# The experts' preparation at the ends of the last layer: by pairs of sequences, or by half sequences

## The chip, the cores and the metric

The kernel runs on one core of one Trainium2 chip. The metric is the device time of one execution in microseconds (us). The kernel before took 1163.84 us, the median of three runs (1162.24 to 1168.53). The profile is of another single execution, which took 1141.5 us.

## What is computed

Eight sequences (B = 8) of 512 tokens with 128 channels pass a modulated LayerNorm, four layers of a Mamba-2 block, a residual, a second modulated LayerNorm and a mixture of experts. Cut to what matters here:

```
h = layernorm(x) * (1 + ca) + sa
for l in range(4):                      # four Mamba-2 layers
    h = h + mamba2(rmsnorm(h), l)       # its scan runs along the 512 tokens
x = x + ga * rmsnorm(h)                 # final norm: scale F
h = layernorm(x) * (1 + cb) + sb        # scale L
normed = rmsnorm(h)                     # scale G
probs = sigmoid(normed @ router_w.T)    # 8 experts, the best 2 of each token
out = shared(normed) + routed(normed, probs)   # two-layer networks, hidden size 512
x = x + gb * out
```

The three scales F, L and G are powers of -1/2 of a mean or a variance over the 128 channels of a token. They, the two norms between them and the modulation are what the change moves.

## The kernel before, in words

**The layers.** A sequence is cut into four chunks of 128 tokens (NC = 4). An item i is one chunk of one sequence in one layer: NI = 128 items, the last layer's sequence b holding items 96 + 4b to 96 + 4b + 3. One loop over t, from -25 to 131, carries all items as a software pipeline written out by hand: in iteration t it does stage k of item t + k for each stage. So item i has its decay rows loaded in iteration i - 4 (`decay_rows`), their difference and mask made on GpSimd in i - 3 (`decay_diff`, L801, and `decay_mask`, L806), its exponential on ScalarE in i - 2, its products weighed on GpSimd in i - 1 (L844, L847), its state decayed on GpSimd in i (L894). `gate` follows in i + 1, `out_scale` and `project_out` in i + 2, and `out_add` in i + 3. The last two take the items by twos: after an odd item `out_scale` makes the gate norm's scale of both chunks (L966 on VectorE, then the power at L967 on GpSimd), and `out_add` (L975, VectorE) adds both projected chunks to the residual h. The new units' projections and convolutions run 16 iterations ahead, so they end at t = 112. From there on `drain` is true.

**The order of the work.** Each engine works through its queue in order, and this order is fixed when the kernel is built: inside the loop on all engines by `manual_schedule`; after the loop on all engines but GpSimd, whose instructions a planner places. Generators (`gens`) hold the side work: each `yield` ends a step. In every iteration each generator takes one step near the end of the iteration; in the drain those with a tuple as key take a further one in `step_pairs`, ahead of `gate`.

**The ends of the layers.** The generator `rejoin(g)` handles a pair of sequences, 2g and 2g + 1, eight chunks. It starts in iteration 106 + 8g, in which `out_add` finishes the pair's last chunks: at t = 106, 114, 122 and 130. In order, and with [128 x 128] pieces unless said otherwise:

- the modulation's rows `md` come by two DMAs on SyncE (L328);
- eight squares with their sums on ScalarE (`mean_squares`, L312), the mean (L316) and the power F;
- eight copies scaled by F on ScalarE (L343), a product with `md` per sequence (L347) and one sum into x (L349) on VectorE;
- statistics on VectorE (L355, L357), the power L, the offset (L365);
- eight scaled and shifted copies on ScalarE (L368), product and sum with `md` on VectorE (L375);
- eight squares (L312) and the power G.

These are 18 steps. In eleven more follow: the rows (eight copies scaled by G, L385), transposes (L394), the router's product (L402), its sigmoid (L424), the choice of two experts and the positions in the experts' lists on VectorE (L427 to L480), and then 16 scatters of 128 rows each are put on a list. `power` (L297 to L305) computes the three powers: on GpSimd in one instruction for pairs 0 and 1, on VectorE in eleven small ones for pairs 2 and 3.

**Scatters and the shared network.** `scatter` (L487) is an indirect DMA from GpSimd's queue, 64 of them for the rows of all tokens. In the drain one is taken from the list per iteration, while t is at most 124; the loop after the layers takes all that are listed. `shared`, stepped by `serve`, computes the shared network (L529 to L562): six steps per sequence as soon as the sequence is routed, one in each iteration of the drain, three in each round after the loop. The rows of pair 0 and 1 lie in a pool of two buffers; a third pair may not take one inside the loop while scatters of pair 0 are listed (`held`), so that pair 2's rows wait for the loop's end.

**After the loop.** Rounds step the remaining generators twice each, list the scatters and `serve` three times. When all four pairs have counted their tokens, `tables` works out which expert owns which tile of 256 rows. Then the experts' loop reads the rows back (L1188) and works through 39 tiles. Its first read waits for the last scatter.

Of the kernel before, what the change touches and what calls it, by code (L numbers as in the profile page):

```python
# [8 lines left out]
F32 = mybir.dt.float32  # L9
I32 = mybir.dt.int32  # L10
AF = mybir.ActivationFunctionType
ALU = mybir.AluOpType
# [3 lines left out]
P = 128  # L16
# [8 lines left out]
def adaln_mamba_moe(  # L25
# [49 lines left out]
    small = ctx.enter_context(tc.tile_pool(name="small", bufs=4))  # L75
    norm = ctx.enter_context(tc.tile_pool(name="norm", bufs=4))
# [13 lines left out]
    hs = {}  # L90
# [16 lines left out]
    unread = const.tile([P, DM], F32, name="unread")  # L107
    mhalf = const.tile([P, 2 * NC], F32, name="mhalf")
# [5 lines left out]
    scb = const.tile([P, B, P], F32, name="scb")  # L114
# [98 lines left out]
    hTs, hp, xp, xs = {}, {}, {}, {}  # L213


    G2 = 2 * NC
# [19 lines left out]
    mods = lists.tile([B, 4, DM], F32, name="mods")  # L236
# [52 lines left out]
    sets = [(b, b + 1) for b in range(0, B, 2)]  # L289
    routed = set()  # L290

    def power(v, name, on_pool):

        n = v.shape[1]
        y = small.tile([P, G2], F32, tag="py", name=f"py{name}")[:, :n]
        if on_pool:
            nc.gpsimd.tensor_tensor(y, v, mhalf[:, :n], ALU.pow)  # L297
            return y
        t = small.tile([P, G2], F32, tag="pt", name=f"pt{name}")[:, :n]
        nc.vector.tensor_single_scalar(t.bitcast(I32), v.bitcast(I32), 1, ALU.arith_shift_right)  # L300
        nc.vector.tensor_scalar(y.bitcast(I32), t.bitcast(I32), -1, 0x5F3759DF, ALU.mult, ALU.add)
        for _ in range(3):
            nc.vector.tensor_mul(t, y, y)
            nc.vector.scalar_tensor_tensor(t, t, -0.5, v, ALU.mult, ALU.mult)
            nc.vector.scalar_tensor_tensor(y, t, 1.5, y, ALU.add, ALU.mult)  # L305
        return y

    def mean_squares(h, eps, name, on_pool):
        n = h.shape[1]
        ss = small.tile([P, G2], F32, tag="pss", name=f"pss{name}")[:, :n]  # L310
        for j in range(n):
            nc.scalar.activation(unread, h[:, j, :], AF.Square, accum_out=ss[:, j : j + 1])  # L312
            if j % NC == NC - 1:
                yield
        v = small.tile([P, G2], F32, tag="pv", name=f"pv{name}")[:, :n]
        nc.vector.tensor_scalar(v, ss, 1.0 / DM, eps, ALU.mult, ALU.add)  # L316
        return power(v, name, on_pool)

    def rejoin(g):


        seqs = sets[g]
        b0, n = seqs[0], len(seqs) * NC
        parts = [slice(i * NC, (i + 1) * NC) for i in range(len(seqs))]
        md = []
        for b in seqs:
            md.append(norm.tile([P, NC, DM], F32, tag="hn", name=f"md{b}"))
            nc.sync.dma_start(  # L328
                md[-1].rearrange("p k d -> p (k d)"), mods[b].rearrange("k d -> (k d)").partition_broadcast(P)
            )  # L330

        def both(k):

            for i, t in enumerate(parts):
                yield t, md[i][:, k, :].unsqueeze(1).to_broadcast([P, NC, DM])

        mine = slice(b0 % 2 * NC, b0 % 2 * NC + n)
        h, xt = (v[b0 // 2].rearrange("p b s d -> p (b s) d")[:, mine] for v in (hp, xp))
        on_pool = g < 2
        rs = yield from mean_squares(h, 1e-5, f"F{g}", on_pool)  # L340
        yield
        for j in range(n):
            nc.scalar.activation(h[:, j, :], h[:, j, :], AF.Copy, scale=rs[:, j : j + 1])  # L343
            if j % NC == NC - 1:
                yield
        for t, m in both(0):
            nc.vector.tensor_mul(h[:, t, :], h[:, t, :], m)  # L347
        yield
        nc.vector.tensor_add(xt, xt, h)  # L349
        yield  # L350
        mv = small.tile([P, G2, 2], F32, tag="pmv", name=f"mvF{g}")[:, :n]
        for i in range(len(seqs)):
            st = small.tile([P, NC, 6], F32, tag="st", name=f"stF{g}_{i}")
            for s in range(NC):
                nc.vector.bn_stats(st[:, s, :], xt[:, i * NC + s, :])  # L355
            for s in range(NC):
                nc.vector.bn_aggr(mv[:, i * NC + s, :], st[:, s, :])  # L357
            yield
        v = small.tile([P, G2], F32, tag="pv", name=f"pvL{g}")[:, :n]
        nc.vector.tensor_scalar_add(v, mv[:, :, 1], 1e-5)  # L360
        rs = power(v, f"L{g}", on_pool)
        if on_pool:
            yield
        off = small.tile([P, G2], F32, tag="poff", name=f"off{g}")[:, :n]
        nc.vector.scalar_tensor_tensor(off, mv[:, :, 0], -1.0, rs, ALU.mult, ALU.mult)  # L365
        yield
        for j in range(n):
            nc.scalar.activation(  # L368
                h[:, j, :], xt[:, j, :], AF.Identity, bias=off[:, j : j + 1], scale=rs[:, j : j + 1]
            )  # L370
            if j % NC == NC - 1:
                yield
        for k in (2, 1):
            for t, m in both(k):
                nc.vector.tensor_tensor(h[:, t, :], h[:, t, :], m, ALU.mult if k == 2 else ALU.add)  # L375
            yield
        rs = yield from mean_squares(h, 1e-8, f"G{g}", on_pool)
        yield

        while scatters and scatters[0][0] in held.get(len(rowpools), [])[:-1]:  # L380
            yield
# [8 lines left out]
        for i, b in enumerate(seqs):  # L390
            t = parts[i]
# [21 lines left out]
        def t3(tag):  # L413
            return f2.tile([P, G2, E], F32, tag=tag, name=f"{tag}{g}")[:, :n]
# [7 lines left out]
        m = n * E  # L422
        p = t3("prob")
# [29 lines left out]
        src, w = before, 1  # L453
        while w < n:
# [3 lines left out]
            src, w = dst, 2 * w  # L458
# [119 lines left out]
    with ExitStack() as actx:  # L578
# [13 lines left out]
        U = NL * B  # L592
        NI = U * NC
        n = NC * NH
# [3 lines left out]
        dV, Ms, xTs, xds, xes, pg, py, st, gs, sqs, po = ({} for _ in range(11))  # L598
# [364 lines left out]
        def out_scale(i):  # L963
            if i % 2:
                rs = small.tile([P, 2], F32, tag="rg", name=f"rg{i}")
                nc.vector.tensor_scalar(rs, po[i // 2][:, 2 * DM : 2 * DM + 2], 1.0 / DI, 1e-5, ALU.mult, ALU.add)  # L966
                nc.gpsimd.tensor_tensor(rs, rs, mhalf[:, 0:2], ALU.pow)  # L967
                po[i // 2] = po[i // 2], rs

        def out_add(i):  # L970
# [22 lines left out]
        gens = {}  # L993
# [9 lines left out]
        for t in range(-NC * LEAD - EARLY, NI + 4):  # L1003
            p = t + NC * LEAD
# [16 lines left out]
            for g, seqs in enumerate(sets):  # L1021
                if t == NC * (U - B) + NC * (seqs[-1] + 1) + 2:
                    gens["pairs", g] = rejoin(g)
            v, j = divmod(p, NC)
            vc, jc = divmod(p - 1, NC)

# [52 lines left out]
            if item(t - 2):  # L1079
                out_scale(t - 2)  # L1080
# [153 lines left out]
    with tc.manual_schedule(engines={*tc.nc.engines} - {mybir.EngineType.Pool}):  # L1234
# [39 lines left out]
        for b in range(B):  # L1274
            both = xbp.tile([P, NX, L], F32, tag="xbc", name=f"y{b}") if b % 2 == 0 else both
# [7 lines left out]
        for b in range(B):  # L1283
# [3 lines left out]
            y = y1[b].rearrange("p (s d) -> p s d", d=DM)  # L1287
# [56 lines left out]
```

## Time and profile before

| what | us |
|---|---|
| median of three runs | 1163.84 |
| profiled execution, its own time | 1141.5 |
| its span, first to last instruction | 1139.8 |
| iteration 100 begins on GpSimd (L801 of item 103) | 672.43 |
| iteration 112 (item 115) | 738.44 |
| iteration 124 (item 127, the last) | 829.88 |
| scale of the last two chunks begins (L966) | 867.70 |
| last `out_add` (L975) | 872.35 |
| last scatter begins | 948.96 |
| first rows read back | 951.97 |

The times of the iterations are read off GpSimd's timeline: L801 of item i is issued in iteration i - 3, and item 127 is its last. Lines of the trace's answers give a start or a duration in us, the engine (PE TensorE, PEld its weight load, DVE VectorE, ACT ScalarE, POOL GpSimd, SP SyncE), the output by its name in the program, and the line of the kernel. A wait reads "engine output line <- releaser: us in all, times, longest". The lines themselves stand in the prediction.

### The profile page before, as it was taken

To read this page: it belongs to the slowest core of one execution; us is meant where nothing else is said; L and a number is where in the kernel's file an instruction comes from. 1 tells how busy PE (TensorE), PEld (TensorE's weight loads), DVE (VectorE), ACT (ScalarE), POOL (GpSimd) and SP (SyncE) were. 2 spreads that over 40 slices of the span, in tenths; PEclk is the share of its full clock that TensorE was granted. 3 is DMA by queue.
4 is the path that set the end of the run, shared out by engine and by line. 5 is a ranking of instruction groups with operands and counts; after the bars stand their busy time and mean duration, and the time that the engine had idled before them with its cause. 6 is when DMAs were issued, how large, how long until landed. Compare 5 with 4: busy or idle time off the path is not lost. (4 is left out here: it accounts for less than half of the span.)

```text
span 1139.8 us, 21562 instructions
## 1 busy us (share of the span) xinstructions
PE 960.9 (84%) x7130; PEld 730.6 (64%) x7130; DVE 855.0 (75%) x2084; ACT 761.4 (67%) x1641; POOL 856.1 (75%) x937
## 2 busy tenths in 40 slices
PE   4757899989999989899998998988666985999995
PEld 1335676767667667676666676666454674888882
DVE  3768888898888978988889889888764652666653
ACT  4766888878888888788878887876624731333320
POOL 6868879898898898988988988879756163555550
PEclk9777999999999999999999999978876996999998
DMA  5141436556466364563332433434201015878756
GB/s 111 5 139 39 138 100 199 138 167 169 137 194 170 115 195 141 169 184 107 111 120 78 141 111 125 130 94 139 84 24 37 11 55 162 218 223 229 221 147 228
DMA packets 134302, 151.19 MB, mean 133 GB/s; under 512 B 22568, under 2 KB 106696, under 8 KB 134192
## 3 DMA queue, kind: packets, MB, share of 16 engines
q1 hardware_dynamic: 127184, 137.91, 41.5%
q0 software_dynamic: 4672, 9.42, 2.4%
q10 hardware_dynamic: 2336, 2.50, 0.7%
q8 instruction: 56, 0.92, 0.3%
q14 instruction: 54, 0.44, 0.1%
HBM read 120.07 MB, written 29.71 MB: 131 GB/s over the span
## 5 line engine op out<-in xcount | busy, mean ns | idle before, releaser
L668 DVE SCALAR_TENSOR_TENSOR xbc<-px,cw,xbc 128x511 f32<-128x511 f32 (+2 forms) x384 | 286.3, 746 | 35.7 <-ACT xbc L658 28.6
L801 POOL TENSOR_TENSOR dV<-dV,cum 128x1024 f32<-128x1024 f32 x128 | 244.7, 1912 | 4.5 <-DMA dV<-crow 4.3
L860 DVE TENSOR_TENSOR dV<-dV,ptx 128x1024 f32<-128x1024 f32 x128 | 155.0, 1211 | 19.7 <-ACT xT L838 19.7
L806 POOL TENSOR_SCALAR_AFFINE_SELECT dV<-dV 128x1024 f32<-128x1024 f32 x128 | 142.2, 1111 | 9.3
L817 ACT ACTIVATE dV<-dV 128x1024 f32<-128x1024 f32 x128 | 134.5, 1051 | 14.8 <-POOL dV L806 14.5
L487 POOL DMA_INDIRECT yg<-y,ix x78 | 84.1, 1078 | 79.4 <-DVE y L1230 64.8
L944 ACT ACTIVATE sq<-g 128x256 f32<-128x256 f32 x128 | 53.0, 414 | 115.5 <-DVE g L940 104.4
L646 PE MATMUL px<-hT,Wi 128*128 128x512 f32 x192 | 103.8, 622 | 15.8 <-DVE xbc L668 14.5
L658 ACT ACTIVATE xbc<-px,cbias,cw 128x512 f32<-128x512 f32 x128 | 98.6, 770 | 14.6 <-PE px L646 13.4
L487 POOL DMA_INDIRECT xg<-row,ix x64 | 63.0, 984 | 50.3 <-ACT hds L529 29.6
L844 POOL TENSOR_TENSOR xd<-xT,dt 128x256 f32<-128x256 f32 x128 | 79.4, 621 | 26.9 <-ACT xT L838 26.5
L869 PEld LDWEIGHTS py<-xbc,st 128*128 128x128 f32 x384 | 58.9, 200 | 61.3 <-issue 47.0
L959 PE MATMUL po<-Wo,g 128*128 128x128 f32 x512 | 89.4, 298 | 0.0
L1212 ACT ACTIVATE hd<-ph,bs 128x256 f32<-128x256 f32 x78 | 32.8, 471 | 83.7 <-PE ph L1206 81.2
L928 PE MATMUL py<-dV,xd 128*32 128x128 f32 x2048 | 84.6, 284 | 0.0
L955 PEld LDWEIGHTS po<-ones,sq 128*128 128x128 f32 x512 | 68.0, 193 | 25.6 <-issue 23.7
L918 PEld LDWEIGHTS py<-xbc,dg 128*128 128x128 f32 x512 | 78.4, 199 | 6.8 <-issue 1.0
L856 PE MATMUL ptx<-xbc 128*128 128x128 f32 x256 | 55.6, 299 | 31.7 <-DVE dV L860 31.3
L918 PE MATMUL py<-xbc,dg 128*128 128x128 f32 x512 | 80.5, 281 | 0.0
L955 PE MATMUL po<-ones,sq 128*128 128x1 f32 x512 | 78.4, 257 | 0.0
L1219 PE MATMUL pe<-w,hd 128*128 128x128 f32 x624 | 75.9, 275 | 0.0
L1206 PE MATMUL ph<-xt,w 128*128 128x256 f32 x312 | 75.5, 386 | 0.0
(252 smaller groups left out, 2342.5 us busy)
## 6 DMA issues: line engine op xcount, KB each, us to landing
dV<-crow SPq DMA_DIRECT2D x128, 512.0 KB, 4.2
w<-in_L_ffn_ew_dram SPq DMA_DIRECT2D x78, 256.0 KB, 3.3
xg<-blank SPq DMA_DIRECT2D x64, 260.0 KB, 4.6
ecum<-crow SPq DMA_DIRECT2D x256, 48.0 KB, 3.2
rows<-xg SPq DMA_DIRECT2D x39, 130.0 KB, 3.7
b<-in_L_ffn_eb_dram SPq DMA_DIRECT2D x39, 64.0 KB, 4.0
x<-in_L_attn_x_dram SPq DMA_DIRECT2D x8, 256.0 KB, 9.4
md<-mods SPq DMA_DIRECT2D x8, 256.0 KB, 4.3
```

What stands on the lines that cost most here:

```text
L487: i = nc.gpsimd.indirect_dma_start(out=to, out_offset=bass.IndirectOffsetOnAxis(ap=ix, axis=0), in_=of, in_offset=None)
L646: nc.tensor.matmul(px[v, k][:, :L], Wi[l][:, c0 : c0 + P], hT[v], start=True, stop=True)
L658: nc.scalar.activation(xbc[v][:, k, :], px[v, k][:, :L], AF.Identity, bias=cbias[:, l, k : k + 1], scale=cw[:, l, k, KT - 1 : KT],)
L668: nc.vector.scalar_tensor_tensor(xbc[v][:, k, d:], px[v, k][:, : L - d], cw[:, l, k, KT - 1 - d : KT - d], xbc[v][:, k, d:], ALU.mult, ALU ...
L801: nc.gpsimd.tensor_tensor(dV[i], dV[i], cums[g][:, h0 : h0 + NH].unsqueeze(2).to_broadcast([P, NH, Q]), ALU.subtract)
L806: nc.gpsimd.affine_select(out=dV[i], in_=dV[i], pattern=[[0, NH], [1, Q]], compare_op=ALU.is_ge, fill=-200.0, base=0, channel_multiplier=-1,)
L817: nc.scalar.activation(dV[i], dV[i], AF.Exp)
L860: nc.vector.tensor_mul(Ms[i], Ms[i], pg.pop(i).unsqueeze(1).to_broadcast([P, NH, Q]))
L918: nc.tensor.matmul(py[i][:, k, :], dg[l][:, k, :], xbc[u][:, k, t], start=False, stop=True, skip_group_check=True,)
L928: nc.tensor.matmul(py[i][j * HD : (j + 1) * HD, k, :], xd[:, h, :], M[:, h, :], start=False, stop=True, skip_group_check=True,)
L955: nc.tensor.matmul(pp[:, 2 * DM + c : 2 * DM + c + 1], sq[:, k, :], ones[:, 0:1], start=(k == 0), stop=(k == NB - 1))
L959: nc.tensor.matmul(pp[:, c * DM : (c + 1) * DM], g[:, k, :], Wo[l][:, k, :], start=(k == 0), stop=(k == NB - 1))
```

## The change

The first two thirds of `rejoin`, up to the power G, become a generator of their own, `half(b, k)`, for two chunks (half a sequence). It starts in the iteration of the `out_add` that finishes these two chunks: half n = 2b + k starts at t = 100 + 2n, for n = 0 to 15. `rejoin(g)` still starts where it did, but first waits until the pair's four halves are `ready`, and then goes on with the rows. A half has eleven steps. Its key is a tuple as well, so that in the drain it takes two per iteration.

In a half, the copies scaled by F and the products with `md` become one VectorE instruction per chunk (`scalar_tensor_tensor`), the sum into x has 256 columns, and so have product and sum with `md`. The small results lie in columns of `scb`, a tile that is free by then. The powers go to GpSimd for sequences 0 to 5 and to VectorE for 6 and 7 (before: 0 to 3, and 4 to 7); the offset is made on GpSimd in two instructions for all sequences (before: one on VectorE). `md` is loaded per sequence with its first half. `out_scale` of the last two odd items (125, 127) takes its power on VectorE.

The core of the diff:

```
+    def half(b, k):
+        if k == 0:
+            mds[b] = norm.tile([P, NC, DM], F32, tag="hn", name=f"md{b}")
+            nc.sync.dma_start(
+                mds[b].rearrange("p k d -> p (k d)"), mods[b].rearrange("k d -> (k d)").partition_broadcast(P)
+            )
+        two = slice(2 * k, 2 * k + 2)
+        h, xt = hs[b][:, two, :], xs[b][:, two, :]
...
+        def power_of(v, name, to=None):
+            if b < B - 2:
+                to = few() if to is None else to
+                nc.gpsimd.tensor_tensor(to, v, mhalf[:, :2], ALU.pow)
+                return to
+            rs = power(v, f"{name}{b}_{k}")
+            if to is not None:
+                nc.vector.tensor_copy(to, rs)
+            return rs
+
+        ss, v = few(), few()
+        sums(ss)
+        yield
+        nc.vector.tensor_scalar(v, ss, 1.0 / DM, 1e-5, ALU.mult, ALU.add)
+        yield
+        rs = power_of(v, "F")
+        yield
+        for j in range(2):
+            nc.vector.scalar_tensor_tensor(
+                h[:, j, :], h[:, j, :], rs[:, j : j + 1], mds[b][:, 0, :], ALU.mult, ALU.mult
+            )
+        nc.vector.tensor_add(xt, xt, h)
+        yield
...
+        for j in range(2):
+            nc.vector.bn_stats(st[:, j, :], xt[:, j, :])
+        for j in range(2):
+            nc.vector.bn_aggr(mv[:, j, :], st[:, j, :])
+        v, off = few(), few()
+        nc.vector.tensor_scalar_add(v, mv[:, :, 1], 1e-5)
+        yield
+        rs = power_of(v, "L")
+        nc.gpsimd.tensor_mul(off, mv[:, :, 0], rs)
+        nc.gpsimd.tensor_scalar_mul(off, off, -1.0)
+        yield
+        for j in range(2):
+            nc.scalar.activation(
+                h[:, j, :], xt[:, j, :], AF.Identity, bias=off[:, j : j + 1], scale=rs[:, j : j + 1]
+            )
+        yield
+        nc.vector.tensor_mul(h, h, both(2))
+        nc.vector.tensor_add(h, h, both(1))
+        yield
+        ss, v = few(), few()
+        sums(ss)
+        yield
+        nc.vector.tensor_scalar(v, ss, 1.0 / DM, 1e-8, ALU.mult, ALU.add)
+        yield
+        power_of(v, "G", scales(b)[:, two])
+        ready.add((b, k))
...
     def rejoin(g):
...
+        while not all((b, k) in ready for b in seqs for k in range(2)):
             yield
...
-                nc.gpsimd.tensor_tensor(rs, rs, mhalf[:, 0:2], ALU.pow)
+                if i < NI - 4:
+                    nc.gpsimd.tensor_tensor(rs, rs, mhalf[:, 0:2], ALU.pow)
+                else:
+                    rs = power(rs, f"g{i}")
...
+            last = t - 3 - NC * (U - B)
+            if 0 <= last < NC * B and last % 2:
+                gens["half", last] = half(last // NC, last % NC // 2)
```

More of the change, by code (lines that the diff above doesn't have):

```diff
@@ L290, in adaln_mamba_moe, with power @@
     routed = set()
-    def power(v, name, on_pool):
+    scratch = scb.rearrange("p b q -> p (b q)")
+    mds, ready = {}, set()
+    def power(v, name):
         n = v.shape[1]
         y = small.tile([P, G2], F32, tag="py", name=f"py{name}")[:, :n]
-        if on_pool:
-            nc.gpsimd.tensor_tensor(y, v, mhalf[:, :n], ALU.pow)
-            return y
         t = small.tile([P, G2], F32, tag="pt", name=f"pt{name}")[:, :n]
@@ L306, in power, with few, both, sums @@
         return y
[L308 to L317, printed above, removed]
+    def half(b, k):
[6 more added lines that the diff above has]
+        h, xt = hs[b][:, two, :], xs[b][:, two, :]
+        at = [24 * (2 * b + k)]
+        def few(w=2):
+            at[0] += w
+            return scratch[:, at[0] - w : at[0]]
+        def both(row):
+            return mds[b][:, row, :].unsqueeze(1).to_broadcast([P, 2, DM])
+        def sums(ss):
+            for j in range(2):
+                nc.scalar.activation(unread, h[:, j, :], AF.Square, accum_out=ss[:, j : j + 1])
+        def power_of(v, name, to=None):
[20 more added lines that the diff above has]
+        yield
+        st = small.tile([P, NC, 6], F32, tag="st", name=f"stF{b}_{k}")
+        mv = few(4).rearrange("p (s m) -> p s m", m=2)
+        for j in range(2):
[9 more added lines that the diff above has]
+        yield
+        for j in range(2):
+            nc.scalar.activation(
[12 more added lines that the diff above has]
+        ready.add((b, k))
@@ L319, in rejoin, with scales @@
+    def scales(b):
+        return scratch[:, 24 * 2 * B + NC * b : 24 * 2 * B + NC * (b + 1)]
     def rejoin(g):
@@ L324, in rejoin @@
         parts = [slice(i * NC, (i + 1) * NC) for i in range(len(seqs))]
[L325 to L357, printed above, removed]
-            yield
-        v = small.tile([P, G2], F32, tag="pv", name=f"pvL{g}")[:, :n]
@@ L360, in rejoin @@
[L360 to L378, printed above, removed]
+        h = hp[b0 // 2].rearrange("p b s d -> p (b s) d")
+        rs = scratch[:, 24 * 2 * B + NC * b0 : 24 * 2 * B + NC * b0 + n]
+        while not all((b, k) in ready for b in seqs for k in range(2)):
+            yield
         while scatters and scatters[0][0] in held.get(len(rowpools), [])[:-1]:
```

## The prediction

> **What bounds the kernel now.** First I read the busy time by stage, cut at the iterations' starts: iterations 92 to 100, 100 to 106, 106 to 112, 112 to 124, 124 to the end of the layers, from there to the last index of the scatters, and to the first rows read back.
>
> ```profile
> core 0: us, PE busy (x) PEld busy (x) DVE busy (x) ACT busy (x) POOL busy (x), PEclk, DMA share, GB/s
> 627.23:672.43 45.20, 41.70 (x355) 31.54 (x353) 39.74 (x85) 38.30 (x77) 39.47 (x44) 1.00 0.35 113
> 672.43:704.17 31.74, 29.36 (x237) 21.72 (x236) 26.70 (x56) 26.75 (x43) 29.04 (x33) 1.00 0.49 154
> 704.17:738.44 34.27, 32.80 (x284) 24.96 (x282) 29.75 (x60) 28.65 (x63) 29.71 (x31) 0.95 0.36 111
> 738.44:803.59 65.15, 50.49 (x415) 40.38 (x414) 56.84 (x132) 44.70 (x123) 58.20 (x55) 0.84 0.41 130
> 803.59:829.88 26.29, 15.57 (x101) 11.24 (x102) 18.05 (x58) 15.63 (x51) 19.91 (x20) 0.81 0.14 48
> 829.88:872.35 42.47, 31.00 (x197) 24.64 (x196) 21.01 (x87) 13.89 (x44) 25.61 (x29) 0.72 0.09 29
> 872.35:928.97 56.62, 48.11 (x262) 34.00 (x263) 30.20 (x146) 36.47 (x96) 21.14 (x22) 0.88 0.08 27
> ```
>
> The reader is to see two regimes. Up to 803.59 VectorE and GpSimd are both busy 84 to 91% of the time, with no room for much more. After that every engine but TensorE has room. Next the chain of waits, in order of time, at the end of the layers:
>
> ```profile
> 872.35 0.61 DVE h L975 x2
> ...
> 880.61 1.28 ACT h L343 x4
> ...
> 909.52 1.28 ACT row L385 x4
> ...
> 928.34 0.70 ACT hds L529
> ...
> 929.32 0.96 POOL xg L487
> ...
> 948.96 3.00 DMA xg<-row,ix
> 951.97 2.10 DMA rows<-xg
> ```
>
> From the last `out_add` to the first rows read back takes 951.97 - 872.35 = 79.6 us, all on pair 3's way: 37 us of preparation (872.35 to 909.52), 20 of routing, 20 of 16 scatters (1.26 us from start to start), 3 until the last has landed. Last, the waits from 872 to 952:
>
> ```profile
> POOL xg L487 <- ACT hds L529: 29.6, 2, 25.6
> ACT row L385 <- DVE pyG L305: 7.9, 2, 7.5
> DVE h L975 <- POOL rg L967: 4.5, 1, 4.5
> ```
>
> GpSimd stands idle for 25.6 us between the scatters of pair 1 and of pair 2, and VectorE loses 4.5 us on the last power, which stood behind scatters (GpSimd's timeline has ten of them from 858.20 on ahead of L967 at 871.57). The rows of pair 2 wait behind that, and PE starves for a bank until 878.55.
>
> **What the Trainium skill says.** "VectorE: DVE Perf Modes", section "The TRN2 errata — SBUF-src ops pay a fixed extra latency per instruction", prices an fp32 sum or product of N columns at (N + 151)/0.96 ns: 691 ns for 512, where the trace has 641 to 1810 (L375, median 686). I take its 424 ns for 256 columns (an estimate), twice for each half where one instruction had 512 or 1024. "GPSIMD Engine Reference", "Specifications", says that GpSimd and VectorE share SBUF interfaces and contend when a VectorE instruction has two SBUF inputs. The trace agrees: L347, two such inputs, took 691 to 2093 ns, and L801 rose from 1.90 to 2.34 us beside it. "Perfetto Trace Analysis", "DMA Instruction — SWDGE (GPSIMD)", says that the end shown for an indirect DMA is that of its descriptors, not of the data: the 3.00 us on the chain after the last 0.96 us scatter are that.
>
> **The change part by part.**
>
> One half costs, by rows of before. VectorE: three small ones at 0.17, two `scalar_tensor_tensor` of 128 columns at 0.31 (L975 has 0.30 to 0.35), three 256-column ones at 0.42, statistics 0.65 (half of L355 and L357, 0.87 + 0.37), one more 0.17: 3.2 us. ScalarE: four squares with their sums at 0.44 (start to start), two copies at 0.41: 2.6. GpSimd: three powers of two columns at 0.70 (L967), product 0.20 and sign 0.23 (L177, L178): 2.5. For b = 6, 7 the powers are on VectorE: 3 x 2.25 = 6.8 more (eleven instructions, 873.07 to 875.32), and 0.43 on GpSimd. The pairs of before cost GpSimd 4.9 each (3 x 1.64) for pairs 0 and 1 only; VectorE 8.2 uncontended, 11 to 13 with the contention seen. ScalarE loses 32 copies, 12 us, all of it beside other work.
>
> *A, t = 100 to 112 (672.4 to 738.4, 66.0 us).* Six halves begin and take a step per iteration. By 112 they have done 12 us on VectorE, 10 on GpSimd, 11 on ScalarE, where before pair 0's first six steps put 2, 1.6 and 7.3. Added: 10 + 8 + 3 = 21 us. How much shows? Pair 0's own steps give the rate: 11 us of them over six iterations went with 34.27 - 31.74 = 2.5 us, or 0.23 per us. So 21 x 0.23 = **+5 us** (0 if they fall in gaps; 10 if VectorE, then 66.5 us busy, is the bound at 88%). The `md` loads, now one per four iterations on SyncE ahead of the decay rows, cost 0.43 us of issue each and land in 4.3; their buffers are long free, and the rows they stand before are wanted three iterations later: nothing, or 0.4 each if that lead were gone.
>
> *B, t = 112 to 124 (738.4 to 829.9, 91.5 us).* GpSimd is busy 78.1. Five powers of 1.64 go (-8.2), the rest of the 12 halves comes (30.4 - 9.8 - 1.8 = 18.8): 88.7 us. Pair 0 is routed 3.5 to 4 iterations sooner (step 29 was at t = 123, is at 119), so up to seven more of its scatters fall here (8.8): at most 97.5. VectorE: 75 us minus 23 (preparation of pairs 0 and 1) plus 21 to 29 for halves and 8.5 for pair 1's routing: 81 to 89. At 94% of GpSimd's time this stage is 94 to 104 us: +3 to +12. I take **+6** (bounds 0 and +18).
>
> *C, t = 124 to the last scale (829.9 to 867.7).* VectorE has 21 of 42 us. Pair 2's preparation and pair 1's routing leave (some 14), the powers of halves 12 to 14 and of `out_scale` come (some 25): 32 us, fits. Seven scatters may have left, among which L894 waited 6.6 us (VectorE's timeline, 837.16), and pair 1's 16 come in. **-3** (bounds -10, +6).
>
> *D, from L966 of items 126 and 127 on (867.70 to 951.97, 84.3 us).* The last scale takes 2.25 us on VectorE in place of 4.5: `out_add` ends at +3.1. Half 15 then needs 1.0 (squares), 2.6 (mean, power), 1.1, 1.0, 2.3, offset 0.9, copies 1.5, 0.9, squares 1.2, 2.6: rows at about +19, where before they began at 909.52, which is +42. Routing, with TensorE working off the shared network between (three serves per round, 7.25 us per six: eight sequences' matmuls from the trace; 24 of them ahead of pair 3's positions, plus 5): index at +37, before +61. This is no longer last. Pair 2 keeps its place (its rows still wait for the end of the loop), but not behind VectorE's stall: with its 11 steps and 15 serves its index is at +22 (before +37, at 905). Then 32 scatters at 1.26 = 40, landing and read 5: rows at +67.5. **-17** (-10 if pair 2's index stays at +29; -22 if only pair 3 counts: 37 + 20 + 5 = 62). All 48 serves done by then: four more fall in the loop, 33 x 1.21 + 6 = 46 us.
>
> Sum: 5 + 6 - 3 - 17 = **-9 us** on the 1141.5 of the profiled execution: 1132.5, a ratio of 0.992. The median shown is 22 us above that execution, a gap that nothing in the page explains; I carry the ratio over: 1163.84 x 0.992 = 1154.6 us. The experts' loop after 952 is untouched.
>
> **The rivals.** Half a per cent, 5.8 us, is about what a measurement of this kernel can tell from no change.
>
> *The halves hide.* A and B grow by 0 to 2 us, as the pieces are shorter and let the items' work between them (a product of 3.54 us for two instructions, at 768.99, is gone); then -20: 1143.5. For it: 46 us of VectorE's 200 are idle from 672 to 872. Against: the two regimes above.
>
> *Pair 2's scatters are last and come no sooner.* If its index stays near 905, at +37, the end is +37 + 40 + 5 = +82, and D gains 2; with +4 from A to C that is +2: 1166. It speaks for it that pair 2's rows keep their place in the program; against it that they stood waiting for VectorE from 868.
>
> *GpSimd is the bound before t = 124* (the slower side). It must then do 66.9 us in A and 97.5 in B, 164.4 us. If it can't exceed the 89% of 738 to 804, A and B last 185 in place of 157.5: +27; C gives back 5, D 14: +8, or 1172. Price: 30 small operations' us against 9.8 before, in a queue which each item passes three times. It decides once the last `out_add` is more than 17 us later.
>
> **How the numbers follow.** The likeliest case, A to D as summed: 0.42, its own range 1147 to 1160. The halves hide: 0.22. Pair 2's scatters: 0.18. GpSimd the bound: 0.18. Faster by over 0.5% are the second and most of the first (0.36): 0.58. Within: 0.06 and most of the third: 0.22. Slower: 0.20. The range goes from 1138 (hidden, and a D of -25) to 1172, the middle of the slower case; about 0.18 lies outside.
>
> **What would show it.** In the profile after: item 127's L801 at about 841 (829.88 before), L975's last at about 878; no wait of it for L967; pair 3's rows within 25 us of it; GpSimd's gap before pair 2's scatters under 15 us; 32 scatters nearly on end; rows at about 943. It is wrong if L975's last is past 889, or if GpSimd idles before pair 3's scatters.

## The result, and the profile after

The changed kernel takes 1193.76 us in the median of 4 runs (1192.64 to 1196.02), the kernel before 1165.78 us beside it (4 runs, 1162.24 to 1168.53): a ratio of 1.0244, 95% interval 1.0208 to 1.0281. It is slower by 28 us, where 9 us less were forecast. The profiled execution of the change took 1192.96 us, span 1190.3, close to its median; that of before lay 24 us below its median, so the two profiles stand 50 us apart where the medians stand 28. The experiments below ran on five chips, beside a kernel before of 1145 to 1147 us (the last two: 1167), and each ratio is to the runs of before beside it.

Busy time by stage in the changed kernel, cut at the same marks as before: iterations 100, 106, 112, 122, 124, the last `out_add`, the last index of the scatters.

```profile
core 0: us, PE busy (x) PEld busy (x) DVE busy (x) ACT busy (x) POOL busy (x), PEclk, DMA share, GB/s
672.56:707.42 34.86, 31.71 (x240) 23.00 (x239) 30.73 (x66) 29.32 (x56) 32.00 (x38) 0.95 0.44 144
707.42:750.77 43.35, 35.98 (x280) 26.52 (x278) 40.15 (x99) 29.81 (x71) 35.98 (x45) 0.88 0.32 101
750.77:842.93 92.16, 63.79 (x452) 50.60 (x452) 70.63 (x189) 47.93 (x134) 77.69 (x94) 0.74 0.31 101
842.93:858.81 15.88, 9.51 (x65) 6.47 (x65) 13.54 (x25) 6.18 (x14) 13.77 (x17) 0.71 0.03 9
858.81:914.08 55.27, 34.61 (x199) 24.60 (x199) 39.72 (x172) 15.64 (x49) 26.62 (x35) 0.69 0.06 21
914.08:976.42 62.34, 44.81 (x247) 33.86 (x248) 30.05 (x164) 24.68 (x61) 16.39 (x20) 0.80 0.05 18
```

All stages but the fourth are longer: 34.9, 43.4, 92.2, 55.3 and 62.3 us, where before had 31.7, 34.3, 65.2, 42.5 and 56.6. The fourth, t = 122 to 124, has 15.9 us in place of 26.3: nine of pair 0's scatters stood in it before, and 14 of the 16 now stand in the third. VectorE, which had 21 of 42 us in the fifth, now has 40 of 55. Next the chain of waits at the end, in order of time, and the waits after the last `out_add`.

```profile
913.91 0.52 DVE h L995 x2
...
924.15 1.17 ACT row L402 x4
...
953.46 14.75 another core or an unknown queue
968.22 0.57 ACT h L550
...
974.71 0.22 PE pos L479 x2
...
1002.79 3.27 DMA rows<-xg
```

```profile
ACT h L550 <- remote: 33.0, 2, 18.3
POOL xg L504 <- DVE ix L497: 18.2, 1, 18.2
DVE rest L489 <- PE pos L479: 17.6, 2, 16.1
```

The long way of pair 3 (37 us of preparation before) is gone from the chain, but GpSimd still stands idle for 18.2 us until pair 2's index is there. The index is what the last step of a pair's routing makes: the positions to which its rows are scattered. A stretch of 14.75 us that no wait of the program explains holds up pair 3's positions as well: ScalarE stands ahead of a `keep` (L550, the copy of a product of the shared network), though the product is done, until pair 2's scatters have landed. That belongs to this execution and not to the change, as the change run again shows.

### The profile page after: what moved, and what is told of

Read it like the earlier page. It is cut to its first block, busy times and chain, and to the rows that moved or that the text cites. A ratio compares the mean times of both kernels' runs of the same rounds, so it can differ in the third digit from the quotient of the medians.

```text
span 1190.3 us, 21787 instructions
## 1 busy us (share of the span) xinstructions
PE 982.5 (83%) x7130; PEld 742.7 (62%) x7130; DVE 897.6 (75%) x2260; ACT 751.4 (63%) x1609; POOL 875.1 (74%) x997
## 4 chain that ended last, share of the span: by engine, by line
DVE 40%; PE 22%; ACT 12%; POOL 12%; issue 6%; DMA 3%; SPq 2%; another core or an unknown queue 1%; POOLq 0%; DVEq 0%; ACTq 0%
DVE xbc L685 13%; DVE dV L877 7%; PE pe L1242 4%; PE ph L1229 3%; DVE g L957 3%; PE px L663 2%; POOL dV L818 2%; DMA rows<-xg 2%; POOL xg L504 2%; DVE h L995 2%; ACT xbc L698 2%; DVE py L920 2%; PE phs L579 1%; PE pz L669 1%
## 5 line engine op out<-in xcount | busy, mean ns | idle before, releaser
L685 DVE SCALAR_TENSOR_TENSOR xbc<-px,cw,xbc 128x511 f32<-128x511 f32 (+2 forms) x384 | 286.2, 745 | 35.8 <-ACT xbc L675 28.7
L818 POOL TENSOR_TENSOR dV<-dV,cum 128x1024 f32<-128x1024 f32 x128 | 243.0, 1898 | 4.5 <-DMA dV<-crow 4.4
L877 DVE TENSOR_TENSOR dV<-dV,ptx 128x1024 f32<-128x1024 f32 x128 | 155.1, 1211 | 19.5 <-ACT xT L855 18.7
L834 ACT ACTIVATE dV<-dV 128x1024 f32<-128x1024 f32 x128 | 134.6, 1051 | 16.2 <-POOL dV L823 15.9
L972 PEld LDWEIGHTS po<-ones,sq 128*128 128x128 f32 x512 | 68.9, 195 | 30.8 <-issue 22.3
```

What stands on the lines that cost most here:

```text
L685: nc.vector.scalar_tensor_tensor(xbc[v][:, k, d:], px[v, k][:, : L - d], cw[:, l, k, KT - 1 - d : KT - d], xbc[v][:, k, d:], ALU.mult, ALU ...
L818: nc.gpsimd.tensor_tensor(dV[i], dV[i], cums[g][:, h0 : h0 + NH].unsqueeze(2).to_broadcast([P, NH, Q]), ALU.subtract)
L834: nc.scalar.activation(dV[i], dV[i], AF.Exp)
L877: nc.vector.tensor_mul(Ms[i], Ms[i], pg.pop(i).unsqueeze(1).to_broadcast([P, NH, Q]))
L972: nc.tensor.matmul(pp[:, 2 * DM + c : 2 * DM + c + 1], sq[:, k, :], ones[:, 0:1], start=(k == 0), stop=(k == NB - 1))
```

## The experiments

All stages below are of profiled executions, in us. A is t = 100 to 112, B is t = 112 to 124, C is t = 124 to the last scale of `out_scale`, D from there to the first rows read back. The last column is the time from the last scale to pair 2's first scatter.

```
run                                   ratio [95%]             A      B      C      D   pair 2
e1  before, scale powers on VectorE   1.0007 [0.999, 1.0023]  65.6   93.7  38.8   82.7  37.0
e5  the change again                  1.0317 [1.0283,1.0352]  77.6  108.1  48.0   77.5  35.3
e2  scale powers back on GpSimd       1.0261 [1.0231,1.0292]  78.8  108.0  45.6   76.1  34.0
e3  rows of pairs 0, 1 later          1.0205 [1.0167,1.0242]  78.2   88.9  54.5   81.1  38.9
e6  no powers on VectorE              1.0174 [1.0132,1.0216]  77.6  108.1  42.0   70.8  28.7
e10 e3 and e6 together                1.0151 [1.0122,1.0179]  77.8   88.8  47.4   82.6  40.5
e7  GpSimd's small ones out           1.0324 [1.0289,1.0359]  80.5  109.6  47.9   77.7  35.6
e8  VectorE's wide ones out           1.0175 [1.0144,1.0206]  74.6  104.1  44.8   77.4  35.3
e9  both out                          1.0136 [1.0108,1.0165]  73.9   98.8  45.3   77.4  35.4
e16 both, and ScalarE's               1.0092 [1.0066,1.0119]  71.1   96.9  45.1   77.1  35.0
e4  halves of pairs 2, 3 alone        1.0143 [1.0105,1.0181]  66.0   98.4  48.8   79.5  37.3
e11 e4, powers on GpSimd              1.0088 [1.0055,1.0120]  66.7   99.2  39.5   86.2  44.1
e12 pair 3 alone, powers on GpSimd    1.0043 [1.0022,1.0064]  65.6   90.8  41.7   85.1  43.0
e15 the change, pair 2 ahead          1.0239 [1.0212,1.0265]  77.6  108.2  48.2   73.9  27.5
e14 e4, pair 2 ahead                  1.0116 [1.0085,1.0148]  65.6   98.7  52.1   75.9  28.9
e13 e11, pair 2 ahead                 1.0237 [1.0207,1.0267]  65.6   99.2  39.5  102.7  39.1
e17 pair 3 alone, powers on VectorE   1.0050 [1.0030,1.0071]  65.7   94.0  48.8   98.4  46.9
e18 e17, pair 2 ahead                 1.0138 [1.0099,1.0176]  66.0   91.5  48.8  107.7  40.0
```

The stages repeat well from chip to chip: A is 77.6 us in e5, e6 and e15, and B is 108.0 to 108.2 in these, in e2 and in the first profile of the change.

**What the change costs, stage by stage.** e1 is the kernel before with one part of the change:

```diff
-                nc.gpsimd.tensor_tensor(rs, rs, mhalf[:, 0:2], ALU.pow)
+                if i < NI - 4:
+                    nc.gpsimd.tensor_tensor(rs, rs, mhalf[:, 0:2], ALU.pow)
+                else:
+                    rs = power(rs, f"g{i}", False)
```

> The kernel before with one part of the change alone: the scale powers of the last four items (two powers of two columns) on VectorE. Theory A (the change's cost lies in the halves and their small operations before t = 124): this part takes the 4.5 us wait of the last out_add away and adds two times 2.25 us of VectorE beside other work, so 0.994 to 1.002 of before. Theory B (VectorE's powers in the last iterations stretch the end): two powers stand ahead of out_add in VectorE's queue, 1.002 to 1.006. A second use: its profile is nearly that of the kernel before, whose profiled execution was 22 us below the median; if engines wait while scatters run, here too, its span shows it (1155 or more), otherwise about 1140.

It is 1.0007: this part alone costs and brings nothing, and the profile (span 1143.3) can stand for before beside the others. e5 is the changed kernel, unedited.

> The changed kernel, unedited, so that its stages can be set beside those of the other runs. If the 12 us in which GpSimd stands idle between the scatters of pairs 2 and 3 (964.7 to 976.7 in the changed kernel's profile, while ScalarE stands 14.7 us ahead of a keep whose product is done) belong to the change, the stage from the last scale to the first rows is about 93 us here as well, and the ratio 1.024 or more; if they belong to that execution, it is 76 to 82 us as in the runs with one part undone, and the stages before it are 78, 108 and 46 to 51 us.

The wait between the scatters of pairs 2 and 3 is gone (0.3 us), D is 77.5, and the ratio is 1.0317: the change costs 35 us here. The interval lies above that of the first runs (1.0208 to 1.0281), so the size of the loss is known to some 0.7% only; the loss itself is not in doubt. The two by stage, e1 first:

```profile
673.41:739.03 65.62, 60.97 (x518) 45.91 (x516) 57.34 (x119) 55.26 (x105) 58.67 (x62) 1.00 0.42 138
739.03:832.76 93.73, 70.19 (x514) 54.98 (x515) 75.74 (x185) 60.18 (x173) 78.02 (x73) 0.80 0.33 100
832.76:871.60 38.84, 26.11 (x182) 20.98 (x181) 22.67 (x98) 13.35 (x42) 20.11 (x22) 0.74 0.07 23
871.60:954.30 82.70, 58.72 (x346) 43.56 (x344) 43.80 (x189) 38.89 (x103) 41.70 (x44) 0.84 0.19 57
```

```profile
675.70:753.30 77.60, 63.69 (x518) 46.64 (x516) 71.48 (x165) 58.88 (x125) 67.97 (x81) 0.98 0.41 127
753.30:861.40 108.10, 75.23 (x517) 57.33 (x517) 85.01 (x213) 54.00 (x147) 91.51 (x110) 0.75 0.27 84
861.40:909.40 48.00, 29.92 (x199) 23.25 (x199) 35.44 (x154) 14.77 (x45) 27.05 (x35) 0.78 0.08 24
909.40:986.90 77.50, 52.01 (x322) 40.65 (x322) 44.37 (x213) 30.20 (x72) 32.27 (x36) 0.85 0.18 51
```

A grew by 12.0, B by 14.4, C by 9.2, and D shrank by 5.3; 2.3 came before t = 100 and 2.7 after the rows, together the 35.3 us between the spans. In A VectorE's 57.3 us became 71.5 and GpSimd's 58.7 became 68.0; both are near 90% of their stage, before and after. Two other causes can be put aside for A. TensorE's granted clock was 0.98 in e5 and 0.91 in the first profile of the change and in e3, and A is 77.6, 78.2 and 78.2. And no wait of GpSimd or VectorE for a DMA is among e5's waits in A and B, so the earlier `md` loads held nothing up there.

**Which engine makes A and B longer?** Three kernels leave work of sequences 0 to 5 out, a fourth more. e7 takes the first two powers and the offset's two instructions from GpSimd:

```diff
+            if b < B - 2 and to is None:
+                return v
...
-        nc.gpsimd.tensor_mul(off, mv[:, :, 0], rs)
-        nc.gpsimd.tensor_scalar_mul(off, off, -1.0)
+        nc.vector.scalar_tensor_tensor(off, mv[:, :, 0], -1.0, rs, ALU.mult, ALU.mult)
```

> Leaves work out: of sequences 0 to 5, the first two powers of each half (the mean's value stands for them), and the offset is one instruction of VectorE in place of two of GpSimd; some 1.8 us of GpSimd less for each of 12 halves. Theory A (GpSimd's queue of small operations stretches t = 100 to 124): of the 27 us by which those iterations grew, 15 or more go, ratio 1.012 or less. Theory B (VectorE is what is full): under 6 us go, ratio 1.018 to 1.024.

Nothing is gained: 1.0324, A 80.5 and B 109.6. GpSimd is busy for 58.5 of the 80.5 us of A, no longer near 90%, so its queue of small operations is not by itself what stretches A. The removal is not a clean one, as the offset goes to VectorE, whose busy time in A and in the first six iterations of B is 6.7 us above e5's. B hides two opposite moves: its first six iterations take 4.7 us more than in e5, its last six 3.2 us less. e8 takes the five wide instructions from VectorE (`scalar_tensor_tensor` twice, the sum into `x`, two modulations):

```diff
-        for j in range(2):
-            nc.vector.scalar_tensor_tensor(
...
-        nc.vector.tensor_add(xt, xt, h)
+        if b >= B - 2:
...
-        nc.vector.tensor_mul(h, h, both(2))
-        nc.vector.tensor_add(h, h, both(1))
+        if b >= B - 2:
```

> Leaves work out: of sequences 0 to 5, the products with the norm's weights, the sum into x and the two modulations, five VectorE instructions of each half and 1.9 us without contention. Theory B (VectorE is what is full, and all that is put on it shows): t = 100 to 112 goes from 79 to about 68 us, t = 112 to 124 falls by 8 or more, ratio 1.008 or less. Theory A (GpSimd's queue): t = 100 to 112 stays above 75, ratio 1.016 to 1.024.

The ratio falls to 1.0175, in the range of the theory that e7 went against; A only falls to 74.6, far from the 68 that the other asked for, B by 4.0 (3.4 of them in its first six iterations) and C by 3.2. Neither is confirmed. e9 has both edits.

> Leaves work out: both what the run without GpSimd's small operations and the run without VectorE's wide ones left out. Theory C (from t = 100 on VectorE and GpSimd are both full, each about 90% of the time, and VectorE's instructions on SBUF stretch while GpSimd works; taking from one leaves the other): t = 100 to 112, 80 and 75 us with one left out, goes to 66 to 70 with both, and t = 112 to 124 from 110 and 104 to 95 to 101. Theory D (what stretches is the order: ScalarE's squares and copies of the halves stand ahead of the items' work and wait): 74 us or more, and 103 or more.

A stays at 73.9, as the order theory said; B falls to 98.8, as the theory of two full engines said. e16 also leaves the first squares and the scaled copies on ScalarE out:

```diff
         ss, v = few(), few()
-        sums(ss)
+        if b >= B - 2:
+            sums(ss)
...
-        for j in range(2):
+        for j in range(2 if b >= B - 2 else 0):
             nc.scalar.activation(
```

> Leaves work out: what the run with both out left out, and of sequences 0 to 5 the first squares and the scaled copies on ScalarE too (2.0 us for each half). If ScalarE is the third engine that sets iterations (those with the silu of a sequence keep it busy for 8 us on end): t = 100 to 112 goes from 74.0 to 68 to 71 us, t = 112 to 124 from 98.8 to 93 to 96, ratio 1.002 to 1.009. If the rest is VectorE's statistics and small operations: 73 to 74.5 and 97 to 99, ratio 1.012 to 1.015.

A is 71.1 and B 96.9, each just outside the range for ScalarE as the third engine; the ratio is 1.0092. So the 12 us of A come off in pieces: 3.0 with VectorE's wide ones, 0.7 more with GpSimd's, 2.9 more with ScalarE's, and 5.5 stay with what is left (statistics, means, the last squares and powers, and their places in the queues). No one engine is shown to be the bound of A. It fits these numbers that each iteration is limited by the engine that it loads most, and that the halves put a piece on every one of them; no run shows it iteration by iteration.

The trace adds why VectorE's pieces are dear. First VectorE's timeline in the change run again (start, us, engine, line, operation), then GpSimd's:

```profile
702.51 1.37 DVE L362 TENSOR_SCALAR scb<-scb 128x2 f32<-128x2 f32 x1
```

```profile
701.96 1.89 POOL L818 TENSOR_TENSOR dV<-dV,cum 128x1024 f32<-128x1024 f32 x1
```

An addition on two columns, 0.17 us elsewhere, ends at 703.88, right after GpSimd's subtraction (703.85). All eleven groups of the halves' VectorE instructions that last over 1 us in this execution end within 0.3 us after a GpSimd instruction does. The Trainium skill has this in "SBUF — State Buffer", "SBUF: two separate sides": the port pair that VectorE and GpSimd share is an exclusive lock, held "for the whole instruction", and the other "fully blocks". So a small operation costs what is left of the wide GpSimd instruction that it meets: in A and B L362 took 0.65 us in the mean of 11, L379 0.60 of 10, L353 (256 columns) 0.66 of 11, and a half about 5.2 us of VectorE (58.6 us for 11 to 12 of them), where 3.2 were counted. GpSimd's own small instructions did not do this, and there the trace differs from "the whole instruction": nine of the two-column instructions of L345, L362 and L379 met only a two-column GpSimd operation or a scatter, and all nine took 0.15 to 0.17 us. It fits that taking GpSimd's small ones out in e7 did not help VectorE.

**Where the scatters stand.** e3 delays the rows of pairs 0 and 1 by eight steps, to the iterations in which they began before:

```diff
         while not all((b, k) in ready for b in seqs for k in range(2)):
             yield
+        for _ in range(8 if g < 2 else 0):
+            yield
```

> The changed kernel, but pairs 0 and 1 begin their rows four iterations later (eight steps), where they began before, so that no more scatters than before stand among the items' operations in GpSimd's queue. Theory A1 (the scatters' place in GpSimd's queue stretches t = 112 to 124): that stage goes from 116 us to under 102, item 127's L818 comes at 845 or sooner, and the time is 1.005 to 1.015 of before. Theory A2 (the halves' own small operations stretch it): the stage stays at 111 to 118 us and the time at 1.02 to 1.03 or longer, as pair 1's scatters then end later.

Item 127's L820 comes at 841.3 and B is 88.9, as the first theory said; the ratio, 1.0205, is in the range of the second, since C takes 6.5 us and D 3.6 of the 19.2 back. Net of that the edit is worth 1.1%, 13 us. It does more than put the scatters back: ahead of item 127's subtraction on GpSimd (the end of B) stand nine scatters in e1, sixteen in e5 and only one in e3. Pair 1's routing leaves B too (VectorE has 74.7 us there, not 85.0), so the 19.2 us are not shown to be the scatters' alone. The last six iterations of B tell more; here they are in e1, e5 and e3:

```profile
781.00:832.76 51.76, 38.55 (x290) 30.14 (x287) 37.05 (x97) 31.03 (x94) 41.17 (x40) 0.83 0.28 90
797.20:861.40 64.20, 41.68 (x255) 31.04 (x255) 45.65 (x112) 24.39 (x66) 52.09 (x59) 0.68 0.21 69
795.60:841.30 45.70, 34.05 (x231) 27.64 (x231) 37.40 (x100) 22.77 (x64) 37.05 (x45) 0.72 0.22 73
```

GpSimd is busy for 80 or 81% in all three, while VectorE's share goes from 71 to 82%: in these three the stretch is as long as GpSimd's work makes it. (e7, which takes GpSimd's small ones out, gets 3.2 us for 5.7 us less work there.) Of the 14.4 us by which B grew, 12.4 lie here. Between e5 and e3 GpSimd's work differs by 15.0 us, which is fifteen scatters of 1.0 us. GpSimd's timeline in e5 shows the worst of these iterations:

```profile
815.69 1.13 POOL L504 DMA_INDIRECT xg<-row,ix  x1 [0.19 <-issue]
816.86 1.91 POOL L818 TENSOR_TENSOR dV<-dV,cum 128x1024 f32<-128x1024 f32 x1
...
831.87 1.03 POOL L504 DMA_INDIRECT xg<-row,ix  x1 [0.17 <-issue]
...
834.31 1.89 POOL L818 TENSOR_TENSOR dV<-dV,cum 128x1024 f32<-128x1024 f32 x1
```

Eight of pair 0's scatters stand between the decay of one item and that of the next, with three powers: that iteration lasts 17.4 us, where the same one lasted 5.5 in e1, and GpSimd waits in it for nothing but the issue of the scatters, 0.2 to 0.3 us each. In e1 such a block (nine scatters, 819 to 832) stands three iterations later and makes that iteration 17.3 us long as well. So the block is not new; what B pays for in e5 is seven scatters more, some 9 us at 1.26 each (an estimate), and the halves' own operations.

By the program the loop takes one scatter per iteration, and the first of pair 0's comes in iteration 120. That makes five until t = 124; the other eleven can only be those that the program takes after the loop, whose place on GpSimd the planner chooses.

**VectorE's powers.** e2 and e6 are the changed kernel with the scale powers, and with all powers, on GpSimd:

```diff
-                if i < NI - 4:
-                    nc.gpsimd.tensor_tensor(rs, rs, mhalf[:, 0:2], ALU.pow)
-                else:
-                    rs = power(rs, f"g{i}")
+                nc.gpsimd.tensor_tensor(rs, rs, mhalf[:, 0:2], ALU.pow)
```

> The changed kernel with the scale powers of the last items back on GpSimd. Theory A (halves before t = 124): the same time as the changed kernel within 0.3%, 1.021 to 1.028 of before, as the powers then wait behind scatters of pair 1 as well. Theory B (VectorE's powers at the end): 4 to 6 us sooner, 1.018 to 1.021.

The ratio, 1.0261, is in the range of the first theory, but 0.6% below e5, the saving that the second expected. Both ranges were set from the ratio of the first runs, so the ratio decides nothing. C and D together are 3.8 us shorter than in e5, 2.4 of them in C. e6 has this edit and one more:

```diff
-            if b < B - 2:
+            if b < B:
```

> The changed kernel with every power on GpSimd: those of sequences 6 and 7 and of the last items' scales too. Theory A (VectorE's powers crowd the iterations from t = 124 on and pair 2's routing): the stage from t = 124 to the last scale goes from 46 to about 40, pair 2's first scatter comes 28 us after the last scale in place of 34, and the ratio is 1.010 to 1.018. Theory B (the powers lie beside waits for scatters of pair 1 in GpSimd's queue, and go from one queue to the other): 1.022 to 1.030.

The ratio is 1.0174, as expected of VectorE's powers: C falls from 48.0 to 42.0, and pair 2's first scatter comes 28.7 us after the last scale. e10 puts e3 and e6 together.

> The changed kernel with two parts mended at once: pairs 0 and 1 begin their rows four iterations later, and every power is on GpSimd. If the two costs add up (14 us for the scatters' place, 16 us for VectorE's powers): ratio 1.003 to 1.009. If they are one cost, the same waits of the last iterations seen twice: 1.013 to 1.020.

At 1.0151 the savings do not add up, as the second case said. D is 82.6 here: the last of pair 1's scatters begins at 912.7, powers of the halves stand behind it in GpSimd's queue, and pair 2's first scatter comes 18 us later.

**Halves where the engines have room.** e4 keeps pairs 0 and 1 as before (`whole` is the preparation of before), and e11 adds the edit of e6:

```diff
-            if 0 <= last < NC * B and last % 2:
+            if NC * 4 <= last < NC * B and last % 2:
...
+        if g < 2:
+            h, rs = yield from whole(g)
-        while not all((b, k) in ready for b in seqs for k in range(2)):
+        while g >= 2 and not all((b, k) in ready for b in seqs for k in range(2)):
```

> Halves for pairs 2 and 3 alone; pairs 0 and 1 are prepared whole as before, and the scale powers of the last items stay on VectorE. Theory A (halves of pairs 0 and 1, or their scatters, on saturated engines): t = 100 to 124 takes 160 to 168 us in place of 186, and if the end gains nothing the time is 0.998 to 1.008 of before, with a gain at the end down to 0.990. Theory B (the cost lies after t = 124: VectorE's powers and engines that wait while scatters run): 1.012 to 1.025.

> Halves for pairs 2 and 3 alone, every power of theirs and of the last scales on GpSimd. t = 100 to 112 as before (66 us). If VectorE's powers were what the last iterations and pair 2's index waited for, t = 124 to the last scale goes from 49 to 41 us and the stage to the first rows from 79.5 to 71, ratio 0.998 to 1.004; otherwise 1.008 to 1.014.

e4 (1.0143) has A as before and loses 4.7 us in B and 10 in C. Its ratio is in the range for costs after t = 124: nearly half of the change's loss is there with A as it was. e11 is 1.0088: C falls to 39.5 as expected, but D rises to 86.2 where 71 were expected. The powers now stand among pair 1's scatters (the last begins at 902.5), and ScalarE, with pair 2's rows in its queue, waits 11.5 us for a half's offset:

```profile
901.02 0.88 ACT L383 ACTIVATE h<-x,scb 128x128 f32<-128x128 f32 x2 [11.48 <-POOL scb L380]
```

Next, e12 has halves for pair 3 alone (`NC * 6`, `g < 3`).

> Halves for pair 3 alone, their powers and the last scales' on GpSimd; pairs 0, 1 and 2 are prepared whole, pair 2's powers on VectorE as before. Until t = 124 nothing but what was before (160 us). If the gain of the end is pair 3's preparation, the stage after the last scale is 68 to 76 us in place of 83, ratio 0.986 to 0.996. If it is pair 2's index that decides the end (its rows begin no sooner, 32 scatters follow), 78 to 84 us and 0.996 to 1.004.

Until t = 124 nothing is lost, and D does not shrink: it is 85.1, just above the range of the second case, with pair 2's first scatter 43.0 us after the last scale ("at +43.0" from here on). The ratio is 1.0043. With nothing paid in A and B there is no gain at the end either.

**What sets the end.** In each of the twelve runs in which pair 3's scatters follow pair 2's at once, the first rows come 42.0 to 42.2 us after pair 2's first scatter. So D is the time to pair 2's first scatter plus 42. Three runs give pair 2's generator two more steps per round after the loop, ahead of the other generators:

```diff
+        second = gens.get(("pairs", 2))
         while tail or serving or scatters or table or not tab:
+            for _ in range(2):
+                if second in tail and not step(second):
+                    tail.remove(second)
             for g in list(tail):
```

> The changed kernel with the same two steps more for pair 2 after the loop, and nothing else. Its halves are ready by then, and its own powers are on GpSimd ahead of all but the last of pair 1's scatters. Theory A: pair 2's first scatter comes 22 to 29 us after the last scale in place of 35, the first rows 42 us after that, ratio 1.018 to 1.026 in place of 1.032. Theory B: 34 us or more, ratio 1.029 to 1.034.

> The run with halves of pairs 2 and 3 alone and the powers of sequences 6 and 7 and of the last scales on VectorE, with the same two steps more for pair 2. Theory A: pair 2's first scatter comes 26 to 32 us after the last scale in place of 37, ratio 1.003 to 1.010. Theory B: 36 us or more, ratio 1.012 to 1.016.

> The run with halves of pairs 2 and 3 alone and all powers on GpSimd, but after the loop pair 2's generator takes two steps more per round, ahead of the halves of pair 3. Theory A (halves of pair 3 stand ahead of pair 2's rows and routing in the queues): pair 2's first scatter comes 27 to 36 us after the last scale in place of 44, and the first rows 42 us after that; ratio 0.994 to 1.003. Theory B (pair 2 waits for its own powers, which stand behind pair 1's scatters on GpSimd): 41 us or more, ratio 1.006 to 1.011.

e15 and e14 show that the order of the generators holds pair 2: +35.3 became +27.5, and +37.3 became +28.9, and e15's ratio, 1.0239, is in the range named for it. Pair 3 comes later for it (5.1 and 6.6 us from the last scatter of pair 2 to its first), so D gains 3.5 and 3.6, not 8. In e14 C is 3.3 us longer than in e4, which is not explained, and its ratio, 1.0116, lies just above the range for the order. ScalarE's timeline in e5 has pair 2's second set of rows 14.2 us after the last scale, that in e15, below it, ahead of the last scale (912.6):

```profile
923.69 1.26 ACT L402 ACTIVATE row<-h,scb 128x128 f32<-128x128 f32 x4
```

```profile
910.05 1.85 ACT L402 ACTIVATE row<-h,scb 128x128 f32<-128x128 f32 x6
```

e13 is 1.0237, outside both ranges: pair 2 came only 5 us sooner, and pair 3's last power went behind pair 2's 16 scatters on GpSimd (938.94 in its timeline). ScalarE's rows waited for it, and 22.3 us opened between the last scatter of pair 2 and the first of pair 3:

```profile
939.70 0.69 ACT L480 ACTIVATE row<-h,scb 128x128 f32<-128x128 f32 x2 [14.53 <-POOL scb L349]
```

e17 and e18 have pair 3's halves alone with its powers on VectorE, e18 with pair 2 ahead.

> Halves for pair 3 alone, its powers on VectorE, the last scales' on GpSimd. If the powers behind pair 1's scatters held pair 2 (e12), its first scatter comes 33 to 38 us after the last scale, the first rows 42 us after it, ratio 0.995 to 1.002. If it is the halves' place in the order, 40 us or more and 1.002 to 1.008.

> The same, and pair 2's generator takes two steps more per round after the loop. If order holds pair 2: its first scatter comes 28 to 33 us after the last scale, the first rows 45 to 48 us after that, ratio 0.992 to 0.999, sooner than before. If pair 2 is limited by its own preparation, which is still whole (37 us before): 35 us or more, ratio 0.998 to 1.004.

They are 1.0050 and 1.0138, with pair 2's first scatter at +46.9 and +40.0: e17 is in the range of its second case, e18 in neither. In both profiles ScalarE stands 6 to 13 us at a time ahead of instructions for nothing that the program shows, while scatters run, so their stage D says little and neither theory is settled by them; C, 48.8 us as in e4, has VectorE's powers in it again. No kernel of this study is faster than the one before.

## Why the prediction was wrong

**A, +5 forecast, +12.0 measured.** The sum of added work was too small and so was the rate. VectorE's time on halves in A was put at 12 us (before 2); the trace has 18.7 (before 1.7), mostly because blocked operations were priced at their free duration. GpSimd's 10.9 was right (10). With ScalarE's 5.7 the added work is 32 us, not 21, and 0.37 us of each showed, not 0.23. The rate had been read off pair 0's first steps, of which two thirds (7.3 of 11 us) were ScalarE's; halves put most of their work on VectorE and GpSimd. That this is why the rate was too low is argued, not shown.

**B, +6 forecast, +14.4.** The busy times were right: VectorE 85.0 (81 to 89 forecast), GpSimd 91.5 (at most 97.5), with the "up to seven more" scatters all there. The step that failed is "At 94% of GpSimd's time". By the prediction's own figures GpSimd was busy for 78.1 of 91.5 us before, 85%, and no reason was given why that share should rise. It did not: 91.5 us in 108.1 are 85% again. Between e1 and e5 GpSimd has 13.5 us more to do in B, and B is 14.4 us longer.

**C, -3 forecast, +9.2.** "32 us, fits" counted VectorE's time in the stage (35.4 measured, of 48.0) and not its place. The powers of halves 12 to 14 are 11 instructions each in a queue in front of the `out_add` on which the next squares wait. e2, with the scale powers on GpSimd, takes 2.4 us off, and e6, with the halves' too, 6.0.

**D, -17 forecast, -5.3.** Half 15 did what was forecast: pair 3's rows begin 23.4 us after the last `out_add` in e5 (936.87), and 32 scatters run on end there. The step that failed is pair 2's index "at +22": it is at +35.3. Its 11 steps and the shared network do take 21 us from its second rows on (923.69 to 944.76), but those rows stand behind pair 3's halves on ScalarE and VectorE for 14 us, which the forecast left at nothing. e15 undoes that order and takes 7.8 us off; e6 takes 6.6 off.

**The rivals.** "GpSimd is the bound before t = 124" had A and B at 185 us; they are 185.7. Part of that is luck. Its price was small operations in a queue at 89%, and in A that fell with e7; it was right for the last six iterations of B, where the stretch follows GpSimd's work, scatters above all. Its gains after t = 124 did not come. "Pair 2's scatters are last and come no sooner" was right on the mechanism of the end: +37 and a gain of 2 forecast for D, +35.3 and 5.3 measured. That both would hold at once was in no case.

Of the signs named: item 127's L818 came at 858.8 (841 forecast), the last L995 at 913.9 (878), GpSimd's gap before pair 2's scatters was 18.2 us (under 15), and both things that were to prove the forecast wrong came in: L995's last past 889, and GpSimd idle before pair 3's scatters (11.1 us in that execution, 0.3 in e5).

What is not settled: the last 5.5 us of A, the 2.8 us by which e7 made A longer, and 3 us of C that are left when every power is on GpSimd.

## What to carry to other kernels

Where two in-order engines are each near 90% busy, work moved in from a later, idle stretch shows at once, and not only on the fuller one: in A, taking GpSimd's part out gave nothing, VectorE's part 3 us of 12. Do not count on an engine to be busier after a change than it was before: B ran at 85% of GpSimd's time both times. Before preparation is moved forward, ask what decides the end (here pair 2's index, then 42 us of scatters), what the moved steps now stand in front of in each queue, and which other work they set free to start. Price VectorE's small SBUF operations at what is left of a wide GpSimd instruction, not at their own length.

## What the runs showed of the hardware that was not expected

Free, L362 takes 0.17 us; beside GpSimd's 1.89 us subtraction it took up to 2.22. Beside GpSimd's two-column power it took 0.17. It has one input in SBUF, not two. The Trainium skill's "GPSIMD Engine Reference", "Specifications", names two inputs or a two-port mode for such contention; the second would fit, but no run here shows which mode it ran in.

While scatters run, other engines can stand still for no wait of the program. In the first profile of the change ScalarE stood 14.7 and 18.3 us until the last scatter of a pair had landed, and TensorE's products and SyncE's instructions went by one per 0.70 us or a multiple of it from 986 to 999. e17 and e18 show the like (12.6 us at most); these three ran beside a kernel before of 1166 to 1167 us. In the other sixteen experiments, on four other chips than e17 and e18 and beside 1145 to 1147 us, no such wait is in the profile. It may make up the 20 us or so between those two levels of the kernel before; no profile of it at the higher level was taken, so this is argued, not shown.
